# One projection for queries and keys, spread by transfers, and one load of the first batch in a two-layer attention kernel

## The chip, the cores and the metric

The kernel runs on one core of a Trainium2 chip, in one launch. The metric is the device time of that core in microseconds, the median of the runs; the profile is one more execution, recorded by the hardware profiler. "Granted clock" is the share of full speed that TensorE was allowed to run at.

## The reference

The input x is [4, 128, 64, 64] in float32: 4 batches of 128 channels by S = 4096 positions. Layer 0 is an attention over 1x1 convolutions with 64 channels for queries and keys:

```python
def _prelu(x, a):
    return jnp.where(x >= 0, x, a * x)
def _conv1x1(x, w, b, a):
    y = jnp.einsum('oc,nchw->nohw', w, x) + b[None, :, None, None]
    return _prelu(y, a)
e1 = _conv1x1(x, w1, b1, a1).reshape(N, -1, HW)     # queries, 64 channels
e2 = _conv1x1(x, w2, b2, a2).reshape(N, -1, HW)     # keys, 64 channels
asm = _conv1x1(x, wa, ba, aa).reshape(N, C, HW)     # values, 128 channels
score = jax.nn.softmax(jnp.einsum('nci,ncj->nij', e1, e2), axis=2)
out = jnp.einsum('nij,ncj->nci', score, asm)
...
x = x + _L0_conv_ref(_gn(x), ...)                   # _gn: group norm, 32 groups
t = _to_tokens(x)
t = t + _L1_attn_ref(_ln_t(t), Wq, Wk, Wv)          # layer 1: attention over tokens, D = 128
t = t + _L1_ffn_ref(_ln_t(t), gate_w, gate_b, weight1, weight2)   # routed experts
x = _from_tokens(t, x)
```

The change lies in layer 0 alone: in the group norm of the first batch, and in how e1 and e2 are made.

## The kernel before, in words

A batch is cut into 8 blocks of 512 positions (`BLK`), and the keys of a batch into 16 pairs of 128-position tiles. Everything is float32.

The work is a row of stages, `stage(b, layer, beside, then, ahead, pace)`, written out by hand at L767 and after: layer 0 of batch 0, layer 0 of batch 1, layer 1 of batch 0, layer 0 of batch 2, and so on. In a stage, `attention(b, layer)` goes over the 8 query blocks n and, for each, over 8 groups g of two pairs of keys. For a group, TensorE makes the scores (`ps`, L482), ScalarE their exponentials (`pt`, L491), and TensorE multiplies the group before with the values (`av`, L416 in layer 0, L444 in layer 1). VectorE adds up the exponentials in layer 0 (`sacc`, L503 and L506) and mixes them for layer 1 (L430 to L432). After the last group `finish_conv` or `finish_attn` ends the block in a few steps: in layer 0 a sum over the keys (`c`, L524; `pd`, L528), a reciprocal (L530), products and sums on GpSimd, and a store to DRAM (L535).

Python generators bring in what later stages need. Each step of `attention` advances one step of `beside` (statistics, keys and values of later batches), at g = 1 and after also the query of the next block (`coming`), and in the first block of queries up to three steps of `ahead`. The tile framework then orders the instructions of each engine and puts in the waits; each engine, and each queue that issues transfers, works through its own list in order.

What the change touches, with lines of the kernel before:

- `group_norm(b)`, L178: loads the 8 blocks of x (`g`, L96), takes statistics of each (`bn_stats`, L182), puts them together (L186), and gets mean and factor of each group of channels by two small products (L189, L199) with short VectorE operations between and after (L168 to L173, L191 to L194).
- `normed`, L215: one VectorE operation, (x - mean) * factor, on a 128x512 block.
- `conv_half`, L219: a product of 128x128 weights with the normalised block (`peq` for queries, `pek` for keys, both L222), and a copy with bias on ScalarE (L226). The 64 output channels stand twice in the weights (`w12`), so that both halves of the 128 partitions hold the same 64 rows.
- `prelu`, L207 and L209: two VectorE steps.
- `conv_keys(b)`, L231: for each block the load (`ck`), `normed`, `conv_half(1, ...)`, and the activation into the key tile `kA`, in two operations that write 64 partitions each: partitions 0 to 63 take the first tile of each pair, partitions 64 to 127 the second. Then four products for the values (`pa`, L256) and their activation into `vT`.
- `conv_query(b, n)`, L273: loads the block (`xq`, which is also the residual that the end of the block adds), `normed`, `conv_half(0, ...)`, activation into `q`.
- In the scores of layer 0 the upper 64 partitions of `kA` meet the upper 64 of `q`, and the lower the lower. That is why the query has to stand in both halves.

Loads go through SyncE's queue, those of the constants through ScalarE's. The loads of x for statistics, keys and layer 1 share four buffers (`xs`); normalised blocks (`xn`), `ye` and `te` have two each; `q` two; `xq` four. The large tiles of a batch (`kA`, `vT`) are in `seq`, two buffers each. The kernel opens with the statistics of batch 0, then the query of its first block, then the first stage, whose `ahead` is `conv_keys(0)` with six steps at once and three for each group.

Of the kernel before, what the change touches and what calls it, by code (L numbers as in the profile page):

```python
# [9 lines left out]
F32 = mybir.dt.float32  # L10
AF = mybir.ActivationFunctionType
# [4 lines left out]
P = 128  # L16
BLK = 512
# [9 lines left out]
def tile_unshifted(  # L27
# [14 lines left out]
    nc = tc.nc  # L42
    x = a["x"]
    B, C, S = x.shape
    E, D1, H = a["weight1"].shape
    O = a["weight2"].shape[2]
    CR = a["w12T"].shape[1] // 2
    assert C == P and D1 == P + 1 and O == P and 2 * CR == P and 2 * E == P and B == 4
    NB = S // BLK
    NJ = S // P  # L50
    SUB = BLK // P
# [5 lines left out]
    const = ctx.enter_context(tc.tile_pool(name="const", bufs=1))  # L57
# [18 lines left out]
    def ms_tile(name):  # L76
        return ps_ms.tile([P, BLK], F32, tag="ms", name=name)

    def block_tile(tag, name, bufs=2):
        pool = pools[of_pool.get(tag, "blk")]  # L80
        return pool.tile([P, BLK], F32, tag=tag, name=name, bufs=bufs)

    def dram_tile(shape, name):
        return dram.tile(shape, F32, tag=name, name=name)
# [6 lines left out]
    tokens = [[dram_tile([P, SUB, C], f"tk_{b}_{n}") for n in range(NB)] for b in range(B)]  # L91
    first_pair = dram_tile([P, S], "first_pair")

    def load_block(tag, src, name, bufs):
        t = block_tile(tag, name, bufs)
        nc.sync.dma_start(out=t, in_=src)  # L96
        return t

    def x_of(b, n):
        return x[b][:, bass.ts(n, BLK)]  # L100


    gn_x = [load_block("xs", x_of(0, n), f"g0_{n}", 4) for n in range(3)]

    def const_load(name, shape, src):
        t = const.tile(shape, F32, tag=name, name=name)
        nc.scalar.dma_start(out=t, in_=src)
        return t

    w12 = const.tile([P, 2, 2, CR], F32, tag="w12", name="w12")  # L110
    a12 = const.tile([P, 2], F32, tag="a12", name="a12")
    b12 = const.tile([P, 2], F32, tag="b12", name="b12")
    for i, al in enumerate(("a1", "a2")):
        for h in range(2):
            half = slice(h * CR, (h + 1) * CR)
            nc.scalar.dma_start(out=w12[:, i, h, :], in_=a["w12T"][:, bass.ts(i, CR)])
            nc.scalar.dma_start(out=b12[half, i : i + 1], in_=a["b12"][bass.ts(i, CR), :])
        nc.scalar.dma_start(out=a12[:, i : i + 1], in_=a[al].partition_broadcast(P))
    wa = const_load("wa_sb", [P, C], a["waT"])
    ba = const_load("ba_sb", [P, C], a["ba"].partition_broadcast(P))  # L120
    aa = const_load("aa_sb", [P, 1], a["aa"].partition_broadcast(P))
# [53 lines left out]

    gn = {}

    def group_norm(b, first=()):  # L178
        st = small.tile([P, NB, 6], F32, tag="gn_st", name=f"gn_st{b}")
        for n in range(NB):  # L180
            xb = first[n] if n < len(first) else load_block("xs", x_of(b, n), f"g{b}_{n}", 4)
            nc.vector.bn_stats(out=st[:, n, :], in_=xb)  # L182
            if n % 2 == 1:
                yield
        mv = small.tile([P, 2], F32, tag="gn_mv", name=f"gn_mv{b}")
        nc.vector.bn_aggr(out=mv, in_=st.rearrange("p n s -> p (n s)"))  # L186
        yield
        pm = ms_tile(f"gn_pm{b}")
        nc.tensor.matmul(pm[:, 0:1], lhsT=avg_g, rhs=mv[:, 0:1], start=True, stop=True)  # L189
        ab = const.tile([P, 2], F32, tag=f"gn{b}", name=f"gn{b}")  # L190
        nc.vector.tensor_copy(ab[:, 0:1], pm[:, 0:1])  # L191
        d = small.tile([P, 2], F32, tag="gn_d", name=f"gn_d{b}")
        nc.vector.tensor_sub(d[:, 0:1], mv[:, 0:1], ab[:, 0:1])
        nc.vector.scalar_tensor_tensor(  # L194
            d[:, 1:2], in0=d[:, 0:1], scalar=d[:, 0:1], in1=mv[:, 1:2], op0=ALU.mult, op1=ALU.add
        )
        yield
        pv = ms_tile(f"gn_pv{b}")
        nc.tensor.matmul(pv[:, 0:1], lhsT=avg_g, rhs=d[:, 1:2], start=True, stop=True)  # L199
        inv_sqrt(ab[:, 1:2], pv[:, 0:1], GN_EPS, 1, f"gn{b}")  # L200
        gn[b] = ab
        yield


    def prelu(outs, y, t, alpha):

        nc.vector.tensor_scalar(t, y, 0.0, alpha, op0=ALU.min, op1=ALU.mult)  # L207
        for o, part in outs:
            nc.vector.scalar_tensor_tensor(  # L209
                o, in0=part(y), scalar=0.0, in1=part(t), op0=ALU.max, op1=ALU.add  # L210
            )

    def normed(b, xb, name):
        xn = block_tile("xn", name)
        nc.vector.tensor_scalar(  # L215
            xn, xb, gn[b][:, 0:1], gn[b][:, 1:2], op0=ALU.subtract, op1=ALU.mult
        )
        return xn

    def conv_half(i, xn, name):  # L220
        pe = ms_tile(f"pe{name}")
        nc.tensor.matmul(  # L222
            pe, lhsT=w12[:, i].rearrange("p h c -> p (h c)"), rhs=xn, start=True, stop=True
        )
        y, t = block_tile("ye", f"ye{name}"), block_tile("te", f"te{name}")
        nc.scalar.activation(y, pe, AF.Identity, bias=b12[:, i : i + 1])  # L226
        return y, t

    keys, values = {}, {}

    def conv_keys(b):  # L231


        kA = seq.tile([P, NP, P], F32, tag="k", name=f"e2_{b}")
        vT = seq.tile([P, NJ, C], F32, tag="v", name=f"asm{b}")
        keys[b, 0], values[b, 0] = kA, vT
        xb = load_block("xs", x_of(b, 0), f"ck{b}_0", 4)
        for n in range(NB):
            xn = normed(b, xb, f"xk{b}_{n}")
            if n + 1 < NB:  # L240
                xb = load_block("xs", x_of(b, n + 1), f"ck{b}_{n + 1}", 4)
            yield
            y, t = conv_half(1, xn, f"k{b}_{n}")
            pairs = bass.ts(n, SUB // 2)

            def piece(h):
                rows = slice(h * CR, (h + 1) * CR)
                return kA[rows, pairs, :], lambda z: z[rows, :].rearrange(
                    "c (p h t) -> c p h t", h=2, t=P
                )[:, :, h, :]  # L250

            prelu([piece(0), piece(1)], y, t, a12[:, 1:2])
            yield
            pa = ms_tile(f"pa{b}_{n}")
            for s in range(SUB):
                nc.tensor.matmul(  # L256
                    pa[:, bass.ts(s, P)], lhsT=xn[:, bass.ts(s, P)], rhs=wa, start=True, stop=True
                )
            y2, t2 = block_tile("ye", f"ya{b}_{n}"), block_tile("te", f"ta{b}_{n}")
            y3 = y2.rearrange("p (s c) -> p s c", c=C)  # L260
            nc.vector.tensor_tensor(
                y3, pa.rearrange("p (s c) -> p s c", c=C),
                ba.unsqueeze(1).to_broadcast([P, SUB, C]), op=ALU.add,
            )
            prelu(
                [(vT[:, bass.ts(n, SUB), :], lambda z: z.rearrange("p (s c) -> p s c", c=C))],
                y2, t2, aa,
            )
            yield
# [2 lines left out]

    def conv_query(b, n):  # L273

        resid[b, 0, n] = xq = load_block("xq", x_of(b, n), f"xq{b}_{n}", 4)
        yield
        xn = normed(b, xq, f"xqn{b}_{n}")
        yield
        y, t = conv_half(0, xn, f"q{b}_{n}")
        q = block_tile("q", f"e1_{b}_{n}")  # L280
        prelu([(q, lambda z: z)], y, t, a12[:, 0:1])
        queries[b, 0, n] = q
        yield


# [395 lines left out]
    def run(gen):  # L681
        for _ in gen:
            pass
# [18 lines left out]
    def chain(*gens):  # L702
        for g in gens:
            yield from g
# [4 lines left out]
    def stage(b, layer, beside, then, ahead=None, pace=(6, 3)):  # L709

        coming = iter(())
        for k in range(pace[0]):
            next(ahead or iter(()), None)
        for n, g in attention(b, layer):
            step_after()
            if g == 1:
                coming = query(b, layer, n + 1) if n + 1 < NB else then and query(*then, 0)
                coming = coming or iter(())  # L720
            next(coming, None)
            if n == 0 and ahead:
                for _ in range(pace[1]):
                    next(ahead, None)
            else:
                next(beside, None)
        run(coming)
        run(beside)

    run(group_norm(0, gn_x))  # L730
    run(query(0, 0, 0))
    def take_from_seq(b):
        def take(what):
# [30 lines left out]
        weights(1, seq, "v")  # L764
        yield

    stage(0, 0, chain(group_norm(1), conv_keys(1), weights_qk()), (1, 0), ahead=conv_keys(0))  # L767
    stage(1, 0, chain(group_norm(2), attn_keys(0), mix_values(0)), (0, 1))
    stage(0, 1, chain(group_norm(3), conv_keys(2)), (2, 0))
    stage(2, 0, chain(done_after(route(0, take_from_seq(0))), attn_keys(1), mix_values(1)), (1, 1))  # L770
    stage(1, 1, conv_keys(3), (3, 0))
    stage(3, 0, chain(done_after(route(1, take_from_seq(1))), attn_keys(2), mix_values(2)), (2, 1))
    stage(2, 1, attn_keys(3), (3, 1))
    ends["prep"].close()
# [672 lines left out]
```

## Time and profile before

| | |
|---|---|
| time, median of 3 | 3559.84 us (3558.11 to 3560.43) |
| span of the profiled execution | 3558.6 us |
| mean granted clock | 0.984 |
| TensorE, first 20 us | 1.26 us busy |
| TensorE, 20 to 3390 us | 18 us idle in all |
| DMA, first 20 us | 216 GB/s |
| DMA, whole span | 40 GB/s |

A page of the profile gives busy time, share of the span and number of instructions of each engine; then the span in 40 slices, each digit a tenth of busy time. Groups of instructions have a line, an engine, an operation, what is written from what, shapes and number; after the bar the busy time, the mean duration in ns, and the idle time of the engine just before them with what ended it. A product in float32 shows as two records. Timelines give start and duration in us.

Where TensorE stands idle between the start and the end, it is in a few places: some 3 us at 58 to 64 us, 6 us at 562 to 571 us, and some 4 us each near 1290 and 2140 us. The last two slices are the experts and the final store, which the change does not touch.

### The profile page before, as it was taken

Reading aid. Unit: us, or ns where it says so; the run is one execution under the profiler, and the core shown is the slowest. Engines: PE = TensorE matmul, PEld = TensorE weight load, DVE = VectorE, ACT = ScalarE, POOL = GpSimd, SP = SyncE. Lnnn points to the kernel's source line nnn. Section 1 sums busy time; section 2 is a strip of 40 time slices with the busy share of each in tenths; the row PEclk is TensorE's granted clock in tenths of the full one; section 3 lists DMA queues with packets and bytes.
Section 4 is the critical chain, followed back from the end, with each engine's and each line's share of the span. In section 5 each row is a group of like instructions: output and inputs, shape, how many; then the busy total and the mean of one; then the engine's idle time right before and its main releaser. Section 6 shows DMA issues by size and latency. Waiting matters only on the chain.

```text
span 3558.6 us, 48815 instructions
## 1 busy us (share of the span) xinstructions
PE 3456.7 (97%) x19968; PEld 1631.2 (46%) x19968; DVE 2175.0 (61%) x4154; ACT 1339.3 (38%) x1555; POOL 508.6 (14%) x394
## 2 busy tenths in 40 slices
PE   7999999999999999999999999999999999999966
PEld 3444444444444445444444445444444444454432
DVE  7686576656665565766655566675665557555543
ACT  2333343333333343433333344443343334333330
POOL 0112243220000022421000003332100003000000
PEclk9999999999999999999999999999999999999977
DMA  3010011000000010100000001110100001010159
GB/s 102 24 48 13 13 36 54 15 15 22 21 19 10 19 39 18 42 24 19 24 16 19 10 19 58 34 34 12 39 22 19 13 16 42 10 66 7 36 197 355
DMA packets 75450, 142.37 MB, mean 40 GB/s; under 512 B 8593, under 2 KB 9361, under 8 KB 74961
## 3 DMA queue, kind: packets, MB, share of 16 engines
q1 hardware_dynamic: 67952, 130.18, 10.9%
q10 hardware_dynamic: 7264, 8.98, 0.7%
q8 instruction: 158, 2.59, 0.3%
q14 instruction: 76, 0.61, 0.1%
HBM read 95.10 MB, written 44.04 MB: 39 GB/s over the span
## 4 chain that ended last, share of the span: by engine, by line
PE 94%; DVE 3%; DMA 2%; ACT 1%; issue 0%; POOL 0%; SPq 0%; ACTq 0%; DVEq 0%; POOLq 0%
PE ps L482 38%; PE av L416 23%; PE av L444 22%; PE l_c L312 1%; DMA g<-in_x_dram 1%; PE pv L562 1%; PE pg L591 1%; PE peq L222 1%; PE pd L528 1%; PE pq L386 1%; PE pa L256 1%; PE pek L222 1%; PE ph L828 1%; PE x_c L312 1%; PE po L858 1%; PE l_t L289 0%
## 5 line engine op out<-in xcount | busy, mean ns | idle before, releaser
L491 ACT ACTIVATE pt<-ps 128x1024 f32<-128x1024 f32 x1024 | 1021.4, 1023 | 1293.6 <-PE ps L482 1214.0
L482 PE MATMUL ps<-q,t 128*64 128x512 f32 x4096 | 936.3, 597 | 0.0
L416 PE MATMUL av<-pt,asm 64*128 64x512 f32 x4096 | 925.8, 591 | 0.9 <-ACT sw L546 0.9
L506 DVE TENSOR_TENSOR sacc<-sacc,pt 128x1024 f32<-128x1024 f32 x448 | 615.5, 1374 | 262.7 <-ACT pt L491 239.9
L430 DVE TENSOR_TENSOR tt<-pt 128x512 f32<-128x512 f32 x512 | 358.2, 700 | 493.7 <-ACT pt L491 474.3
L444 PE MATMUL av<-pt,tt 128*64 128x256 f32 x3072 | 636.5, 379 | 0.0
L416 PEld LDWEIGHTS av<-pt,asm 64*128 64x128 f32 x4096 | 405.6, 188 | 480.3 <-issue 466.6
L444 PE MATMUL av<-tt,mixed 128*64 128x256 f32 x2048 | 525.9, 380 | 0.0
L482 PEld LDWEIGHTS ps<-q,t 128*64 128x64 f32 x4096 | 281.2, 137 | 519.3 <-issue 479.6
L482 PE MATMUL ps<-e,e 64*128 64x512 f32 x2048 | 505.0, 611 | 7.2 <-ACT pt L491 7.1
L444 PEld LDWEIGHTS av<-pt,tt 128*64 128x64 f32 x3072 | 352.6, 137 | 289.4 <-issue 142.2
L169 POOL TENSOR_TENSOR l_y<-l_v,mhalf 128x4 f32<-128x4 f32 x64 | 74.3, 1161 | 1758.2 <-DVE l_v L168 1757.9
L444 PE MATMUL av<-tt,tt 128*64 128x256 f32 x1024 | 304.9, 380 | 0.0
L444 PE MATMUL av<-pt,mixed 128*64 128x256 f32 x1024 | 304.6, 379 | 0.0
L482 PEld LDWEIGHTS ps<-e,e 64*128 64x128 f32 x2048 | 190.9, 189 | 234.8 <-issue 216.2
L444 PEld LDWEIGHTS av<-tt,mixed 128*64 128x64 f32 x2048 | 280.8, 137 | 2.4
L431 DVE TENSOR_TENSOR pt<-tt,pt 128x256 f32<-128x256 f32 x512 | 220.0, 430 | 14.8
L432 DVE TENSOR_TENSOR tt<-pt 128x256 f32<-128x256 f32 x512 | 220.2, 431 | 14.2
L444 PEld LDWEIGHTS av<-pt,mixed 128*64 128x64 f32 x1024 | 139.4, 137 | 72.1
L444 PEld LDWEIGHTS av<-tt,tt 128*64 128x64 f32 x1024 | 140.3, 137 | 1.7 <-DVE tt L432 0.2
L530 DVE RECIPROCAL inv<-pd 128x512 f32<-128x512 f32 x32 | 107.4, 3356 | 36.9 <-PE pd L528 36.9
L525 POOL TENSOR_TENSOR all_sum<-all_sum,c 128x512 f32<-128x512 f32 x32 | 46.1, 1440 | 532.2 <-DVE c L524 532.2
(192 smaller groups left out, 2167.1 us busy)
## 6 DMA issues: line engine op xcount, KB each, us to landing
w<-in_weight_dram SPq DMA_DIRECT2D x32, 1024.0 KB, 12.0
x<-xp SPq DMA_DIRECT2D x64, 256.0 KB, 2.2
g<-in_x_dram SPq DMA_DIRECT2D x32, 256.0 KB, 2.8
xq<-in_x_dram SPq DMA_DIRECT2D x32, 256.0 KB, 3.1
ck<-in_x_dram SPq DMA_DIRECT2D x32, 256.0 KB, 2.9
ak<-x SPq DMA_DIRECT2D x32, 256.0 KB, 2.8
xT<-xT SPq DMA_DIRECT2D x32, 256.0 KB, 2.9
xr<-xT SPq DMA_DIRECT2D x32, 256.0 KB, 2.7
```

Of the source, the lines that this page charges most:

```text
L169: nc.gpsimd.tensor_tensor(y[:, :k], v[:, :k], mhalf[:, :k], op=ALU.pow)
L222: nc.tensor.matmul(pe, lhsT=w12[:, i].rearrange("p h c -> p (h c)"), rhs=xn, start=True, stop=True)
L312: nc.tensor.transpose(pt[:, bass.ts(s, P)], src[:, s, :], ident)
L416: nc.tensor.matmul(avs[b, 0, n][:, r, :], lhsT=values[b, 0][rows, j, :], rhs=pt[rows, h, :], start=(j == 0), stop=(j == NJ - 1),)
L430: nc.vector.tensor_sub(tt[:, 0:2, :], p4[:, :, 1, :], p4[:, 0, :, :])
L431: nc.vector.tensor_add(p4[:, 0, 1, :], tt[:, 1, :], p4[:, 0, 0, :])
L432: nc.vector.tensor_sub(tt[:, 2, :], p4[:, 1, 0, :], p4[:, 0, 1, :])
L444: nc.tensor.matmul(av[bass.ts(half, HC), bank, slot, :], lhsT=lhsT, rhs=rhs, start=first, stop=final, skip_group_check=True,)
L482: nc.tensor.matmul(ps[part, h, :], lhsT=key[:, part], rhs=q[rows, :], start=True, stop=True,)
L491: nc.scalar.activation(pt, ps, AF.Exp, scale=scale)
L506: nc.vector.tensor_add(sums[b, n], sums[b, n], pt)
L530: nc.vector.reciprocal(r, pd)
```

## The change

The queries and the keys of a block come from one product: the weights now hold w1 in columns 0 to 63 and w2 in columns 64 to 127, so partitions 0 to 63 of the product are the query and 64 to 127 the key. One ScalarE copy with bias and one activation follow for both (`b12` and `a12` hold one value for each partition). The halves that attention needs are then made by transfers from SyncE's queue: two from the key half of `ye` into the two halves of `kA`, and one of the query half to a DRAM tile `e1[b][n]`, from which `conv_query` later loads both halves of `q`. The second normalisation, product, copy and activation per block go.

For batch 0, x is loaded once as a whole into a buffer of `seq`, in four parts on two queues, and serves the statistics and the projections; before, the statistics and the keys each loaded their own blocks. The first three steps of `conv(0)` (block 0) now run ahead of the first query, and the first stage then takes three steps at once instead of six.

```diff
+    e1 = [[dram_tile([CR, BLK], f"e1_{b}_{n}") for n in range(NB)] for b in range(B)]
...
-    gn_x = [load_block("xs", x_of(0, n), f"g0_{n}", 4) for n in range(3)]
+    first_x = seq.tile([P, S], F32, tag="v", name="first_x")
+    for i, q in enumerate((nc.sync, nc.scalar, nc.sync, nc.scalar)):
+        part = bass.ts(i, S // 4)
+        q.dma_start(out=first_x[:, part], in_=x[0][:, part])
...
+    w12 = const_load("w12", [P, 2 * CR], a["w12T"])
+    b12 = const_load("b12", [P, 1], a["b12"])
+    a12 = const.tile([P, 1], F32, tag="a12", name="a12")
...
-    def group_norm(b, first=()):
+    def group_norm(b, first=None):
...
-            xb = first[n] if n < len(first) else load_block("xs", x_of(b, n), f"g{b}_{n}", 4)
+            if first is None:
+                xb = load_block("xs", x_of(b, n), f"g{b}_{n}", 4)
+            else:
+                xb = first[:, bass.ts(n, BLK)]
...
-            y, t = conv_half(1, xn, f"k{b}_{n}")
...
-            prelu([piece(0), piece(1)], y, t, a12[:, 1:2])
+            pe = ms_tile(f"pe{b}_{n}")
+            nc.tensor.matmul(pe, lhsT=w12, rhs=xn, start=True, stop=True)
+            y, t = block_tile("ye", f"ye{b}_{n}"), block_tile("te", f"te{b}_{n}")
+            nc.scalar.activation(y, pe, AF.Identity, bias=b12)
+            prelu([(y, lambda z: z)], y, t, a12)
+            y4 = y[CR:, :].rearrange("c (p h t) -> c p h t", h=2, t=P)
+            for h in range(2):
+                nc.sync.dma_start(
+                    out=kA[h * CR : (h + 1) * CR, bass.ts(n, SUB // 2), :], in_=y4[:, :, h, :]
+                )
+            nc.sync.dma_start(out=e1[b][n], in_=y[:CR, :])
...
-        resid[b, 0, n] = xq = load_block("xq", x_of(b, n), f"xq{b}_{n}", 4)
-        yield
-        xn = normed(b, xq, f"xqn{b}_{n}")
-        yield
-        y, t = conv_half(0, xn, f"q{b}_{n}")
-        q = block_tile("q", f"e1_{b}_{n}")
-        prelu([(q, lambda z: z)], y, t, a12[:, 0:1])
-        queries[b, 0, n] = q
+        resid[b, 0, n] = load_block("xq", x_of(b, n), f"xq{b}_{n}", 4)
+        queries[b, 0, n] = q = block_tile("q", f"e1_{b}_{n}")
+        for h in range(2):
+            nc.sync.dma_start(out=q[h * CR : (h + 1) * CR, :], in_=e1[b][n])
...
-    run(group_norm(0, gn_x))
+    run(group_norm(0, first_x))
+    first_conv = conv(0, first_x)
+    for _ in range(3):
+        next(first_conv)
     run(query(0, 0, 0))
...
-    stage(0, 0, chain(group_norm(1), conv_keys(1), weights_qk()), (1, 0), ahead=conv_keys(0))
+    stage(0, 0, chain(group_norm(1), conv(1), weights_qk()), (1, 0), ahead=first_conv, pace=(3, 3))
```

In the other stages `conv_keys(b)` becomes `conv(b)` in the same place.

## The prediction

> **What bounds the kernel now.** I read the page's busy table and its 40 slices first, then the groups of instructions on TensorE, the waits of TensorE between 51 and 3390 us, and last the timeline at the start and around single products. The page, with TensorE's row of the slices:
>
> ```profile
> span 3558.6 us, 48815 instructions
> PE 3456.7 (97%) x19968; PEld 1631.2 (46%) x19968; DVE 2175.0 (61%) x4154; ACT 1339.3 (38%) x1555; POOL 508.6 (14%) x394
> ...
> PE   7999999999999999999999999999999999999966
> ```
>
> TensorE is full in every slice but the first and the last two. VectorE (61%) and ScalarE (38%) have room in every stage. So an instruction taken off TensorE between those ends is worth its whole time, and one taken off another engine nothing, unless TensorE was waiting for it. The waits of TensorE from 51 to 3390 us (waiter, engine waited for, us in total, times, longest) say where it was:
>
> ```profile
> PE ps L482 <- ACT pt L491: 7.1, 2, 3.6
> PE pd L528 <- DVE c L524: 4.1, 1, 4.1
> PE pek L222 <- DVE xk L215: 1.9, 1, 1.9
> ```
>
> The whole answer sums to some 18 us. What the change removes, in the groups on TensorE (64 records are 32 products; the last column is the idle time before them):
>
> ```profile
> L222 PE MATMUL peq<-xqn,w 128*128 128x512 f32 x64 | 36.6, 654 | 2.3 <-DVE xqn L215 2.3
> ```
>
> Busy time counts overlap with the next product, so I price a product by the start of what follows it. The timeline of TensorE (start, us, ...) shows one query product alone between value products (av) and scores (ps), a step without one, and a query product beside a key product:
>
> ```profile
> 50.32 1.13 PE L222 MATMUL peq<-xqn,w 128*128 128x512 f32 x2
> 51.28 1.02 PE L222 MATMUL pek<-xk,w 128*128 128x512 f32 x2
> ...
> 97.50 3.60 PE L416 MATMUL av<-pt,asm 64*128 64x512 f32 x16
> 100.93 1.88 PE L482 MATMUL ps<-e,e 64*128 64x512 f32 x8
> 102.65 3.60 PE L416 MATMUL av<-pt,asm 64*128 64x512 f32 x16
> 106.18 1.13 PE L222 MATMUL peq<-xqn,w 128*128 128x512 f32 x2
> 107.23 1.99 PE L482 MATMUL ps<-e,e 64*128 64x512 f32 x8
> ```
>
> From av to ps takes 3.43 us without it (97.50 to 100.93) and 4.58 with it (102.65 to 107.23): 1.15 us. Beside another full product it is 51.28 - 50.32 = 0.96 us.
>
> The start, the other thing that the change touches, in the timeline of all engines:
>
> ```profile
> 15.27 0.37 DVE L186 BATCH_NORM_AGGREGATE gn_mv<-gn_st 128x2 f32<-128x48 f32 x1
> ...
> 19.28 0.55 DVE L215 TENSOR_SCALAR xqn<-xq,gn 128x512 f32<-128x512 f32 x1
> ...
> 26.51 1.99 PE L482 MATMUL ps<-e,e 64*128 64x512 f32 x8
> ```
>
> The statistics end at 15.3 us, the first normalised block is there at 19.8, the first score starts at 26.51. A second hole follows, in TensorE's timeline:
>
> ```profile
> 60.66 1.92 PE L222 MATMUL pek<-xk,w 128*128 128x512 f32 x2 [1.93 <-DVE xk L215]
> 63.47 2.07 PE L256 MATMUL pa<-wa_sb,xk 128*128 128x128 f32 x8 [0.89 <-DVE ya L261]
> 65.48 3.04 PE L482 MATMUL ps<-e,e 64*128 64x512 f32 x8
> ```
>
> Here VectorE stood in batch 1's statistics, waiting for their loads. The usual step is pek 0.96, pa 0.98, ps 1.82; here it ran from 58.66 to 68.35, 9.7 us for 3.8: some 6 us lost.
>
> **What the Trainium skill says.** "TensorE: Matmul & The Clock Gate", section "What's actually happening": after an idle window of about 3.4 us TensorE falls to half its clock until it has been busy for as long. The trace agrees: the slow records above follow idle time, and after the 4.1 us wait for c at 562 us a score group shows 3.79 us instead of 1.99. "DMA: Bandwidth & Descriptors", section "Anatomy of one DMA", has about 2.0 us fixed for a transfer and says that semaphore waits are taken on the issuing sequencer; the trace has 2.2 us for a 256 KB store (x from xp) and 2.8 to 3.1 for a load, so I use those. The same page, "Issuing engines are not separate DMA queues": a second issuing queue saves issue time, not bandwidth. The trace moves 190 GB/s in the first 10 us and 242 in the next, with single slices to 374, so I expect no doubling.
>
> **The change part by part.** *Query products.* 32 leave. The key product keeps its shape (128x128 weights, 512 columns) and its price. Leaving out blocks 0 and 1 of batch 0, which belong to the start below, 30 go. By their neighbours in the order of TensorE, of the 24 behind the first that I looked through, 13 stand alone and 11 beside another product; in that proportion, with block 1 among the latter, I take 17 at 1.15 and 13 at 0.96: 19.6 + 12.5 = **32.0 us**. Ends: 30 x 0.96 = 28.8 and 30 x 1.15 = 34.5.
>
> *Other engines.* VectorE loses per block a normalisation (0.54), the two steps of the activation (0.49 + 0.69) and 0.86 - 0.69 for the halves of the key; ScalarE loses 0.69. Hidden behind TensorE, so nothing.
>
> *Spread of keys and queries.* Per block SyncE now issues two key transfers, a store of the query half and later two loads of it: three or four tenths of a us each to issue, landing in 2.2 to 3 us. Keys of batches 1 to 3 are used a stage later and queries about 45 us after their load can start (their slot is free when the scores of two blocks before are done), so both hide. In the first block of batch 0 the key of block n is needed about one step later: from the start of its product to the scores that use it are a whole step and two products, 7.3 + 2 = 9.3 us; key product, ScalarE and VectorE took 4.05 us (35.73 to 39.78), issue and landing 3: 7 of 9.3. Hidden. The buffer of y is now held until three transfers have read it, so ScalarE's copy for a later block waits on SyncE's queue, and the exponentials and then TensorE stand behind it. SyncE's queue is in order and has stores in it that wait for GpSimd; by the order of the built kernel the worst place (batch 1, block 3, behind a store of block 2's output) has about 3 us to spare. I count 0, and up to 10 us (one hole like that at 562 us) for the range.
>
> *Start.* Batch 0 is loaded once, in four 512 KB parts, without waiting for buffers: 2.1 MB at 190 to 370 GB/s after 2.8 us land at about 8.5 to 13 us; I take 10.5, so the eighth statistic ends at 11.5 (before: 15.2). But the built order puts four loads and statistics of batch 1 inside the chain that makes the mean and the factor on VectorE: one ahead of the aggregate, one ahead of the copy of the mean, two ahead of the variance. Each stands behind first_x and two residual blocks in SyncE's queue. Issued from 10.5 us and landing in about 3.3, each pair behind the one before: 13.8 and 14.8, then 16 and 18.3. Aggregate at 14.9, copy 15.6, variance 19.2; the rest takes 1.6 as before (17.67 to 19.28), so the first block is normalised at 21.5 (before 19.8). Three more statistics of batch 1 stand before the activation of block 0 (24.1), then ya, xk, te, ta and ye at 0.69, 0.54, 0.49, 0.49, 0.69 with gaps: 27.4. The query store goes out third, lands at 30.9. Its loads stand in SyncE's queue behind the keys of block 1, whose activation ends at about 30.9 as well; issued at 31.8, landed at 34.6. **First score at about 35 us, 8.5 later.** TensorE idles from 27.8 to 31.6 in it and may be cold again.
>
> On the other side, by then two key and one value product more are done (2 x 0.96 + 0.98 = 2.9 us), the query product of block 1 is gone (0.96), and the hole at 58 to 68 us is gone, because batch 1's statistics are done (6). I add 2 us for the second pair of scores, which wait for exponentials behind a held y. From the first score to the first score of block 1 the old kernel takes 79.08 - 26.51 = 52.6 us; the new one 52.6 - 6 - 2.9 - 1.0 + 2 = 44.7, so it arrives at 79.7 against 79.08. **Sum for the start: +0.6 us.** Ends: loads and statistics landing without waits, first score at 30, -4.4; each load 1 to 2 us later, first score at 41, +6.6.
>
> *Sum:* 3559.84 + 0.6 - 32.0 = 3528.4; I say 3529.
>
> **The rivals.**
> 1. *The start gains outright:* one load instead of two, statistics done 4 us sooner, and batch 1's loads in time. First score at 26.5 with the hole gone: -8 in place of +0.6, 3520. For it: the DMA rate above 300 GB/s in single slices. Against: the order of VectorE, which now mixes two batches.
> 2. *Holes from held buffers and SyncE's queue:* one to two holes of 6 to 10 us, as at 58 and 562 us, in the stages that make keys: 3535 to 3548. For it: both old holes come from just such loads ahead of compute on an in-order engine. Against: the 3 us and more to spare counted above.
> 3. *Nothing comes of it:* three to four such holes eat the 32 us: 3552 to 3567.
> 4. *Slower:* the round trip of each query block lands on the path. A store and a load are 2.2 + 2.8 = 5 us; if only half showed on each of 32 blocks, 80 - 32 = +48: 3608. Against: each is issued about a block (some 45 us) ahead. If only batch 0's eight blocks showed it all, 40 - 32 = +8: 3568.
>
> **How the numbers follow.** The forecast has 0.62, rival 1 0.14, rival 2 0.14, rival 3 0.05 (most of it within 0.2%), rival 4 0.05. 0.2% is 7 us, so forecast and rivals 1 and 2 all count as faster: with a little of 3, 0.91; same 0.04; slower 0.05. The range runs from 3518 (rival 1 with 34.5 saved) to 3543 (rival 2 with one and a half holes); it leaves out about 0.13, the worse part of 2, and 3 and 4.
>
> **What would show it.** Right: 32 matmuls of 128x512 fewer on TensorE and a busy time some 30 us lower; no wait for the loads of batch 1 at 58 us; waits of TensorE in the middle still near 18 us; the first score between 30 and 41 us; the first score of block 1 at 75 to 86. Wrong: TensorE waiting for e1, e2 or y in the middle, groups of scores at 3 to 4 us after them, or ScalarE's first activations waiting for transfers after 80 us; then the held buffer is the term that I missed. A first score past 41 us would put the miss into the start.

## The result, and the profile after

The changed kernel takes 3535.3 us (median of four, 3534.6 to 3536.2) beside 3559.9 us before (3558.1 to 3560.4): 24.6 us less, ratio 0.9932 with a 95% interval of 0.9915 to 0.9949. Forecast were 3529.0 us and a range of 3518 to 3543.

The page of the changed kernel, with TensorE's row of the slices:

```profile
span 3533.4 us, 48826 instructions
PE 3421.0 (97%) x19904; PEld 1623.1 (46%) x19904; DVE 2115.3 (60%) x4026; ACT 1318.9 (37%) x1523; POOL 518.3 (15%) x394
...
PE   7999999999999999999999999999999999999965
```

TensorE has 64 records (32 matmuls) less and is 35.7 us less busy. It is still the bound. Its waits between 51 and 3365 us in the changed kernel (waiter, engine waited for, us in total, times, longest):

```profile
PE ps L483 <- ACT pt L492: 7.9, 3, 3.6
PE pd L529 <- DVE c L525: 4.8, 1, 4.8
PE pa L261 <- DVE ya L266: 3.4, 1, 3.4
PE l_c L313 <- DVE tt L305: 3.4, 4, 1.7
...
```

With two small ones more they sum to 21.6 us, against 18.0 before. The two waits in the hole at 58 us (1.9 and 0.9) are gone; the wait of 3.4 us of pa for ya is new, and the waits for tt, pt and c are 3.0 us longer together. The products that are left, in the groups, and TensorE's timeline at the place where a query product stood alone before, with the row that follows that query product in the kernel before:

```profile
L248 PE MATMUL pe<-xk,w 128*128 128x512 f32 x64 | 37.4, 667 | 4.7 <-DVE xk L222 2.7 <-ACT ye L250 1.2 <-DVE ya L266 0.8
```

```profile
103.59 3.60 PE L417 MATMUL av<-pt,asm 64*128 64x512 f32 x16
107.03 1.88 PE L483 MATMUL ps<-e,e 64*128 64x512 f32 x8
108.74 3.60 PE L417 MATMUL av<-pt,asm 64*128 64x512 f32 x16
```

```profile
109.06 3.60 PE L416 MATMUL av<-pt,asm 64*128 64x512 f32 x16
```

From av to ps are 3.44 us, where 4.58 were; and the next value products follow the scores after 1.71 us, where after a query product they followed after 1.83 (107.23 to 109.06). So from one group of value products to the next are 5.15 us, where 6.41 were, and a product alone is worth 1.26 us.

The start in the timeline of the changed kernel:

```profile
12.64 0.35 DVE L193 BATCH_NORM_AGGREGATE gn_mv<-gn_st 128x2 f32<-128x48 f32 x1
...
19.69 1.00 DVE L222 TENSOR_SCALAR xk<-first_x,gn 128x512 f32<-128x512 f32 x2
...
35.27 3.02 PE L483 MATMUL ps<-e,e 64*128 64x512 f32 x8
```

**Where the time went.** Each query block of layer 0 ends with one product pd, and each of layer 1 with pg. The start of these 64 products, matched between the two traces, tells how far the changed kernel has come ahead. The first five:

| end of query block | before, us | after, us | difference | step |
|---|---|---|---|---|
| batch 0, block 0 | 94.62 | 95.57 | +0.95 | |
| block 1 | 140.62 | 140.31 | -0.31 | -1.26 |
| block 2 | 189.92 | 188.75 | -1.17 | -0.86 |
| block 3 | 240.87 | 243.57 | +2.70 | **+3.87** |
| block 4 | 290.74 | 292.58 | +1.84 | -0.86 |

From block 4 on it gains mostly in steps of 0.86 or 1.26 (in the two blocks that end at 563 and 613 us it loses 0.54 and gains 2.82, together about the worth of two products), stands still where a stage has no query product to lose, and ends at -25.67 (3418.37 and 3392.70 for the last product pg). The sum: +0.95 at the start; 16 products alone at 1.26 and 14 beside another at 0.87, -32.3; a new hole in block 3, where a gain of 1.26 was due and 3.87 were lost, +5.1; two places (1494 and 2334 us) where a step was only 0.16 and 0.14, because TensorE waited 0.55 us for tt instead, +1.4; and some small ones, -0.8, of which 0.65 in the block that ends at 1307 us, where no query product was. So 0.95 - 32.3 + 5.1 + 1.4 - 0.8 = -25.65.

The hole, in VectorE's and then TensorE's timeline of the changed kernel:

```profile
210.03 0.68 DVE L189 BATCH_NORM_STATS2 gn_st<-g 128x6 f32<-128x512 f32 x1
215.80 0.69 DVE L189 BATCH_NORM_STATS2 gn_st<-g 128x6 f32<-128x512 f32 x1 [5.09 <-DMA g<-in_x_dram]
...
216.82 0.63 DVE L266 TENSOR_TENSOR ya<-pa,ba_sb 128x512 f32<-128x512 f32 x1
```

```profile
217.50 1.37 PE L261 MATMUL pa<-wa_sb,xk 128*128 128x128 f32 x8 [3.42 <-DVE ya L266]
218.80 3.41 PE L483 MATMUL ps<-e,e 64*128 64x512 f32 x8
```

VectorE stands 5.09 us in the eighth statistic of batch 2, and ya, which frees the PSUM tile for the next value half, stands behind it. TensorE waits 3.42 us, and its next scores run at 3.41 us instead of 1.99. The kernel before had the same wait on VectorE, but with ya ahead of it, and there it cost nothing:

```profile
200.94 0.68 DVE L261 TENSOR_TENSOR ya<-pa,ba_sb 128x512 f32<-128x512 f32 x1
...
211.88 0.69 DVE L182 BATCH_NORM_STATS2 gn_st<-g 128x6 f32<-128x512 f32 x1 [2.79 <-DMA g<-in_x_dram]
```

In the changed kernel ScalarE also stood, in its copy to y, for the spread that still read the buffer:

```profile
213.35 0.69 ACT L250 ACTIVATE ye<-pe,b 128x512 f32<-128x512 f32 x1 [7.99 <-DMA e<-ye]
```

And the load of that statistic was the last of a row on SyncE: the store of x1 waits for GpSimd (xp ends at 209.02), the spread of block 3, a residual block, then the load:

```profile
209.05 0.33 SPq L536 DMA_DIRECT2D x<-xp  x1
209.42 1.32 SPq L254 DMA_DIRECT2D e<-ye  x2
210.79 0.61 SPq L257 DMA_DIRECT2D e<-ye  x1
211.44 0.58 SPq L98 DMA_DIRECT2D xq<-in_x_dram  x1
212.12 0.39 SPq L98 DMA_DIRECT2D g<-in_x_dram  x1
```

The row holds the load back by 1.4 us and not by more: the load also needs a buffer, and that comes free when the seventh statistic ends, at 210.71. The five statistics loads before it (186.39 to 200.48) were each issued 0.02 to 0.03 us after a statistic had ended.

So two theories: A, the held y stalls ScalarE, its exponentials and so TensorE (the prediction's mechanism); B, the late load stalls VectorE and with it ya. B has two parts, the row in the queue and the place of the statistic on VectorE.

### The profile page after: what moved, and what is told of

Its sections match the earlier page's. It is cut to its first block, busy times and chain, and to the rows that moved or that the text cites. A ratio compares the mean times of both kernels' runs of the same rounds, so it can differ in the third digit from the quotient of the medians.

```text
span 3533.4 us, 48826 instructions
## 1 busy us (share of the span) xinstructions
PE 3421.0 (97%) x19904; PEld 1623.1 (46%) x19904; DVE 2115.3 (60%) x4026; ACT 1318.9 (37%) x1523; POOL 518.3 (15%) x394
## 4 chain that ended last, share of the span: by engine, by line
PE 92%; DMA 3%; DVE 2%; ACT 1%; POOL 1%; issue 0%; SPq 0%; ACTq 0%; DVEq 0%; POOLq 0%
PE ps L483 38%; PE av L417 23%; PE av L445 22%; DMA g<-in_x_dram 1%; PE l_c L313 1%; PE pv L563 1%; PE pg L592 1%; PE pa L261 1%; PE pd L529 1%; PE pe L248 1%; PE pq L387 1%; DMA y<-x 1%; PE x_c L313 1%; PE pp L656 0%; PE l_t L290 0%; DMA w<-in_weight_dram 0%
```

## The experiments

The kernels below ran in three groups (1 to 4, 5 to 8, 9 to 11), each beside the kernel before, with medians of 3558.0, 3558.6 and 3557.5 us for it. So times of different groups are compared to about 2 us; where less matters I use the ends of query blocks. The changed kernel and the runs that alter only the order, the queue or the products later on end block 0 at 94.2 to 96.0 us, and runs 1 and 6, which have the same start as each other, at 93.0 and 95.3. So some 2 us there is scatter.

**1. y in buffers of its own** (theory A against B).

```diff
-            y, t = block_tile("ye", f"ye{b}_{n}"), block_tile("te", f"te{b}_{n}")
+            y, t = block_tile("ye", f"ye{b}_{n}"), block_tile("te", f"te{b}_{n}", 1)
...
-            y2, t2 = block_tile("ye", f"ya{b}_{n}"), block_tile("te", f"ta{b}_{n}")
+            y2, t2 = block_tile("ya", f"ya{b}_{n}", 1), block_tile("te", f"ta{b}_{n}", 1)
...
```

Here and below `...` stands for lines of an edit that are left out. y keeps two buffers; y2 now has one of its own, and the temporaries of both share one.

> The changed kernel with y in two buffers of its own (y2 and the two temporaries share the rest), so that the spread no longer holds a buffer that the value half needs. Question: what made the new hole of 5.1 us at 214 to 222 us (query block 3 of batch 0). Theory A, the held y stalls ScalarE and so the exponentials: the hole is gone, 3530 us (3529 to 3532). Theory B, VectorE stands in the eighth statistic of batch 2, whose load is queued on SyncE behind a store that waits for GpSimd and behind the spread; the order on both engines is not touched here: the hole stays, 3534 to 3537 us.

Measured: 3534.1 us (3531.4 to 3536.5). ScalarE no longer waits for a transfer there, it waits for TensorE, in ScalarE's and then TensorE's timeline and wait list of this kernel:

```profile
206.20 0.69 ACT L250 ACTIVATE ye<-pe,b 128x512 f32<-128x512 f32 x1 [3.40 <-PE pe L248]
...
218.81 1.02 ACT L492 ACTIVATE pt<-ps 128x1024 f32<-128x1024 f32 x1 [9.60 <-PE ps L483]
```

```profile
PE pa L261 <- DVE ya L266: 3.2, 1, 3.2
```

The hole is there as before; block 3 even takes 1.2 us longer. Theory A falls.

**2. The store of x1, the residual loads and the spread from GpSimd's queue** (the stores everywhere, the loads from batch 0's fifth block, the spread from batch 1 on), so that the statistics loads stand in a row on SyncE.

```diff
-    resid[b, 0, n] = load_block("xq", x_of(b, n), f"xq{b}_{n}", 4)
+    resid[b, 0, n] = load_block(
+        "xq", x_of(b, n), f"xq{b}_{n}", 4, nc.gpsimd if b or n > 3 else None
+    )
...
-    nc.sync.dma_start(out=x1[b][n], in_=xp)
+    nc.gpsimd.dma_start(out=x1[b][n], in_=xp)
...
+    queue = nc.gpsimd if b else nc.sync
...
```

`queue` then issues the three transfers of the spread.

> The changed kernel with layer 0's stores of x1, its xq loads (from the fifth on) and the spread of batches 1 to 3 issued from GpSimd's queue instead of SyncE's. The eight statistics loads of batch 2 then stand one after another on SyncE with nothing ahead that waits. Theory B (the load is late): the hole at 214 to 222 us is gone, 5.1 us, 3530 us (3528 to 3532). Theory A (y is held): y comes free no earlier, rather later, as its transfer now stands behind GpSimd's additions: hole as before or larger, 3535 to 3540 us. Third possibility, GpSimd's additions get late by issuing: new waits on xp in layer 0, slower than 3540.

Measured: 3537.9 us. The hole shrinks by 3.8 us (block 3 takes 51.05 us, 54.82 in the changed kernel), the wait of pa to 1.3 us:

```profile
PE pa L262 <- DVE ya L267: 1.3, 1, 1.3
```

The 1.3 that is left is VectorE still standing 3.29 us in the eighth statistic: its load was issued at 208.98, when the statistic before it had just ended (208.95) and freed the buffer, and landed 3.2 us later. So the queue is not all of it: the order on VectorE leaves the last load no time. The total gets worse, because 7.6 us are lost again later, 3.1 of them in one block at 2286 to 2334 us, where TensorE waits 2.1 us for tt and runs slow after it (shown in the last section). GpSimd's timeline shows why. It computes `l_y`, from which VectorE makes tt, and now does so behind the issues:

```profile
1454.55 0.63 POOL L539 DMA_DIRECT2D x<-xp  x1 [0.30 <-POOL xp L538]
1455.18 0.55 POOL L98 DMA_DIRECT2D xq<-in_x_dram  x1
1455.74 1.03 POOL L173 TENSOR_TENSOR l_y<-l_v,mhalf 128x4 f32<-128x4 f32 x1
```

In the changed kernel `l_y` follows the addition to xp at once. Here it comes 1.5 us later, and at this place TensorE waits 2.10 us for tt instead of 0.55.

**3. The same, with the spread left on SyncE.**

```diff
-    queue = nc.gpsimd if b else nc.sync
+    queue = nc.sync
```

> As the one before, but the spread stays on SyncE, so that the load of the eighth statistic stands behind the spread of block 3 alone and no longer behind GpSimd's addition. Theory B in its full form (store and spread each cost their part): the load is issued 2 to 2.5 us earlier, the hole shrinks to 2.5 to 3 us, 3532.5 to 3533.5 us. If the store alone is to blame: as the one before, 3530. If the store plays no part: 3535.

Measured: 3544.6 us, against 3532.5 to 3533.5 expected, a miss. The load was issued at 210.83, 1.3 us earlier than 212.12, not 2 to 2.5, and the hole shrank by 0.9 us; the wait of pa is 2.7 us. SyncE's queue and VectorE in this kernel:

```profile
209.40 0.60 SPq L258 DMA_DIRECT2D e<-ye  x1
210.83 0.33 SPq L98 DMA_DIRECT2D g<-in_x_dram  x1
```

```profile
210.13 0.68 DVE L189 BATCH_NORM_STATS2 gn_st<-g 128x6 f32<-128x512 f32 x1
215.25 0.69 DVE L189 BATCH_NORM_STATS2 gn_st<-g 128x6 f32<-128x512 f32 x1 [4.44 <-DMA g<-in_x_dram]
```

The queue was free from 210.00, and the load went out 0.02 us after the seventh statistic ended (210.81). So here, as in run 2, it waited for its buffer and for nothing in the queue. It then took 4.4 us to land, where it took 3.2 in run 2; why was not tested. The rest is lost later, in the same blocks as in the run before (8.0 us from the end of block 3 on), though the spread is back on SyncE. So those losses come with the store and the residual loads on GpSimd.

**4. The query products back on TensorE alone**, 30 of them, into PSUM tiles that nobody reads.

```diff
+        if b or n > 1:
+            spare = ms_tile(f"pq{b}_{n}")
+            nc.tensor.matmul(spare, lhsT=w12, rhs=resid[b, 0, n], start=True, stop=True)
...
```

> The changed kernel with the 30 query products of blocks beyond the first two put back on TensorE alone: each product of 128x128 with the residual block goes to a spare PSUM tile that nobody reads; no activation, no VectorE work, no transfer comes with it, and the result is not used. Theory (the gain is TensorE's time): 30 x (0.87 to 1.26) = 26 to 38 us slower than the changed kernel, about 3535 + 32 = 3567 us (3562 to 3572). Rival (a third or more of the gain came from the VectorE, GpSimd and ScalarE work that went with the products): at most 3557 us.

Measured: 3569.2 us, 33.9 more than the changed kernel, as expected. The timeline shows the product's price:

```profile
103.03 3.60 PE L422 MATMUL av<-pt,asm 64*128 64x512 f32 x16
106.56 1.12 PE L288 MATMUL pq<-xq,w 128*128 128x512 f32 x2
107.61 1.99 PE L488 MATMUL ps<-e,e 64*128 64x512 f32 x8
109.43 3.60 PE L422 MATMUL av<-pt,asm 64*128 64x512 f32 x16
```

Again 4.58 from av to ps. In the ends of query blocks nearly all steps are 1.26 and 0.85 to 0.91 as before; the large exception is block 3, +7.3, where the same hole is larger (a wait of 7.1 us for ya: the spare tile takes its turn in the two PSUM tiles that these products share, so the product before the value half has to wait for ya already). So some 6 of the 33.9 us are the hole. Beside the kernel before, the ends of all blocks but block 0 and block 3 keep their steps to 1.6 us in all. So the gain is TensorE's time; for what VectorE and ScalarE were spared, 1.6 us outside these two blocks are left at most.

**5. One edge of order on VectorE:** the eighth statistic of batch 2 behind the value half of block 3 of batch 1.

```diff
-            nc.vector.bn_stats(out=st[:, n, :], in_=xb)
+            with tc.issue_after(last_prelu[1, 3]) if (b, n) == (2, 7) else nullcontext():
+                nc.vector.bn_stats(out=st[:, n, :], in_=xb)
```

`last_prelu[1, 3]` is the instruction that ends that value half on VectorE; the edge sets the order alone.

> The changed kernel with one edge of order on VectorE: the eighth statistic of batch 2 is issued behind the value half of block 3 of batch 1 instead of ahead of it. Two instructions change places, queues and buffers stay. Theory B in the form that the runs so far leave (VectorE stands in a statistic whose load comes late, and y2 stands behind it): the hole at 214 to 222 us is gone altogether, 3530 us (3529 to 3531.5). If the late load also held up something else (the spread, ScalarE's wait of 8 us for y): a hole of 2 us or more stays, 3532 to 3535 us.

Measured: 3531.5 us (3529.7 to 3531.6). VectorE and ScalarE in this kernel:

```profile
210.37 0.68 DVE L190 BATCH_NORM_STATS2 gn_st<-g 128x6 f32<-128x512 f32 x1
210.97 0.67 DVE L268 TENSOR_TENSOR ya<-pa,ba_sb 128x512 f32<-128x512 f32 x1
...
216.09 0.69 DVE L190 BATCH_NORM_STATS2 gn_st<-g 128x6 f32<-128x512 f32 x1 [2.87 <-DMA g<-in_x_dram]
```

```profile
213.70 0.69 ACT L252 ACTIVATE ye<-pe,b 128x512 f32<-128x512 f32 x1 [7.93 <-DMA e<-ye]
```

ya comes at 210.97 instead of 216.82, TensorE has no wait at all between 203 and 224 us, and block 3 takes 5.12 us less: the whole hole. ScalarE waits for y as long as before (7.93), and it costs nothing. That settles it: B, and in B the place of the statistic on VectorE. The load goes out as late as before, behind the same row (212.47), and costs nothing. Of the 5.1 us, 0.9 are lost again in the block that ends at 613 us (the cause was not looked for); the last block ends 3.1 us earlier than in the changed kernel, and the medians, of two groups, are 3.8 us apart.

**6. Both: the edge and y's own buffers.**

```diff
-            y, t = block_tile("ye", f"ye{b}_{n}"), block_tile("te", f"te{b}_{n}")
+            y, t = block_tile("ye", f"ye{b}_{n}"), block_tile("te", f"te{b}_{n}", 1)
+            with tc.issue_after(last_prelu[1, 3]) if (b, n) == (2, 7) else nullcontext():
```

> The edge of order and y's own buffers together. The own buffers brought 1 to 2.5 us at the start (93.0 against 95.6 us at the end of query block 0, of which one us or so can be scatter) and gave 1.2 us back in the hole that the edge removes: 3528 us (3526.5 to 3530). If the gain of the own buffers was scatter: as the edge alone, 3530.

Measured: 3531.4 us, as the edge alone. The gain at the start of run 1 (93.0 us at the end of block 0) is not repeated (95.3); it was scatter. So holding y costs nothing that these runs can measure.

**7. The first load alone**, both products kept, and **8. one product and the spread alone**, with the old loads of batch 0.

```diff
# 7, against the kernel before
-    gn_x = [load_block("xs", x_of(0, n), f"g0_{n}", 4) for n in range(3)]
+    first_x = seq.tile([P, S], F32, tag="v", name="first_x")
+    for i, q in enumerate((nc.sync, nc.scalar, nc.sync, nc.scalar)):
+        part = bass.ts(i, S // 4)
+        q.dma_start(out=first_x[:, part], in_=x[0][:, part])
...
# 8, against the changed kernel: the same lines the other way round
```

> The kernel before with only the first load changed (batch 0 loaded whole by two queues, used for statistics and key blocks); the two products per block stay. The prediction's working has the hole at 58 to 68 us, 6 us, go with this part: 3553 to 3555 us, and the end of query block 0 at 88 to 90 us instead of 94.6. Rival (the start is bound by VectorE and ScalarE, not by the loads): 3557 to 3560 us.

> The changed kernel with the old loads of batch 0 (three blocks for statistics ahead, the others and the projection blocks one by one); one product per block and the spread stay. If the first load is worth 6 us at the start: 3541 us, and the end of query block 0 near 101 us. If it is worth nothing once the query products are gone: 3534 to 3537 us. The 32 us of the products stay in both.

Measured: 3554.95 us for the load alone (ratio 0.9991, 0.9982 to 1.0000), 3540.1 for the product alone (0.9950, 0.9933 to 0.9966); 3541 was expected for the product alone. The ends of block 0, where 88 to 90 us were expected for run 7 and some 101 for run 8:

| | two products | one product and spread |
|---|---|---|
| old loads | 94.62 (before) | 102.74 (run 8) |
| whole first load | 91.88 (run 7) | 95.57 (changed) |

The whole load is worth 2.7 us with the old products and 7.2 with the new one; the single product with its spread costs 8.1 us at the start without the load and 3.7 with it. In run 8 the hole at 58 us is back and a wait for the query's loads with it, in TensorE's timeline:

```profile
34.15 5.29 PE L477 MATMUL ps<-e,e 64*128 64x512 f32 x12 [1.30 <-DMA e<-e]
...
62.18 1.87 PE L255 MATMUL pa<-wa_sb,xk 128*128 128x128 f32 x8 [1.54 <-DVE ya L260]
64.95 4.32 PE L477 MATMUL ps<-e,e 64*128 64x512 f32 x8 [0.90 <-ACT ye L244]
```

In run 7 there is no wait of TensorE from 27 to 75 us. Beside the scatter of some 2 us, the 2.7 us are small, the others are not. So at the start the load pays for most of the latency that the spread brings. In the whole times the two parts nearly add: 3.7 us less for the load and 18.5 for the product, 22.2 together, against 24.6 for both. Run 7 has no hole in block 3 and run 8 has one of 3.2 us, so the hole came with the one product and its spread and not with the load. Whether by the transfers or by the new order on VectorE, these two runs don't tell apart.

**9 to 11. What sets the new start.** All three with the edge of run 5. In 9 the first query tile is filled straight from y, without the way through DRAM; in 10 batch 1's statistics are issued behind the first normalisation of batch 0; 11 has both.

```diff
# 9: the first query
+            if b == 0 and n == 0:
+                queries[0, 0, 0] = q0 = block_tile("q", "e1_0_0")
+                for h in range(2):
+                    nc.gpsimd.dma_start(out=q0[h * CR : (h + 1) * CR, :], in_=y[:CR, :])
...
# 10: every statistic of batch 1
+            behind = {2: last_prelu.get((1, 3)) if n == 7 else None, 1: last_prelu.get("xk")}.get(b)
+            with tc.issue_after(behind) if behind else nullcontext():
+                nc.vector.bn_stats(out=st[:, n, :], in_=xb)
...
+        last_prelu.setdefault("xk", ins.ins)
```

`last_prelu["xk"]` is the first normalisation, of block 0 of batch 0.

> The edge of order of the eighth statistic, and the first query tile alone filled by two transfers straight from y on GpSimd's queue instead of a store to DRAM and two loads back. The first score waited for those loads (issued 30.8 us, first score 35.3 us). If the round trip through DRAM sets the start: first score at 31 to 32 us, and the gain of 3 us or so kept to the end, 3528 us. If VectorE's chain of the next blocks sets it: first score earlier by some us, end of query block 0 within 1 us of the run without, 3530.5 to 3532.

> The edge of order of the eighth statistic, and batch 1's statistics issued on VectorE behind the first normalisation of batch 0. Four of them stood in the chain to the first product in the changed kernel (12.0, 14.7, 16.2 and 17.5 us). If they delay the start: first product at 16.5 to 18 us instead of 20.3, and 2 to 4 us less in all, 3528 us. If the hole at 58 to 68 us comes back, because batch 1's scales come late: 3531 to 3537.

> The edge of order with both changes of the start, the direct first query and the late statistics of batch 1. If both causes add: 3 + 3 us off the edge alone, 3525.5 us (3524 to 3528). If one of the two hides the other: 3528. If the start is bound elsewhere: 3531.

| run | first product | first score | end of block 0 | time, us |
|---|---|---|---|---|
| 5, edge alone | 20.62 | 35.68 | 95.97 | 3531.5 |
| 9, direct query | 19.32 | 29.08 | 90.12 | 3527.3 (3526.1 to 3529.7) |
| 10, late statistics | 15.63 | 31.37 | 91.32 | 3526.1 (3526.0 to 3526.2) |
| 11, both | 15.83 | 25.89 | 92.23 | 3524.3 (3521.9 to 3526.7) |

Run 9 gains 4.2 us on run 5 and run 10 5.4, and both end block 0 more than the scatter earlier (5.9 and 4.7 us). So both the way through DRAM and the four foreign statistics were on the path of the start. Whether they add is not settled. By the medians, which are of two groups, run 11 gains 7.2 of the 9.6 us, with four times from 3521.9 to 3526.7. The execution that was profiled is the slowest of these. In it the first score is 10 us earlier than in run 5, but TensorE waits before it, and its first two groups of scores take 5.19 and 3.79 us instead of 1.99:

```profile
24.22 1.13 PE L253 MATMUL pe<-xk,w 128*128 128x512 f32 x2 [1.81 <-ACT ye L255]
25.89 5.19 PE L492 MATMUL ps<-e,e 64*128 64x512 f32 x8 [0.54 <-DMA e<-ye]
31.01 2.07 PE L271 MATMUL pa<-wa_sb,xk 128*128 128x128 f32 x8
33.01 3.79 PE L492 MATMUL ps<-e,e 64*128 64x512 f32 x8
```

With 3524.3 us (ratio to before 0.9904, 0.9887 to 0.9920) run 11 is the fastest, 11 us below the changed kernel; against run 10 it can't be told apart (the times overlap).

## Why the prediction was right, and where it was not

The time lies in the range and 6.3 us above the forecast. By its steps:

*Query products: right, the size in part by luck.* 32.0 us were forecast, 32.3 found. The two prices erred in opposite ways: alone 1.15 forecast and 1.26 found, because the value products that follow the next scores also come some 0.1 us later after such a product; beside another product 0.96 forecast and 0.87 found. That the saving lies on TensorE is shown by run 4.

*Other engines: nothing, right.* Run 4 puts back TensorE's part only, and outside blocks 0 and 3 all but 1.6 us of the saving goes.

*Start: +0.6 forecast, +0.95 found,* within the scatter of some 2 us. The hole of 6 us that should go went: run 7 has its first score 3.2 us later than before (29.68 against 26.51) and ends block 0 2.7 earlier, so 5.9. The first score came at 35.27, forecast about 35, but partly by luck. The chain on VectorE was faster than worked out (aggregate 12.6 and not 14.9, first normalised block ready by 20.3, when its product starts, not 21.5; the loads of the query issued at 30.8, not 31.8). In its place TensorE, in order, did a value half at 2.05 us and a key product at 2.07 before the score, both at about half their usual speed (1.05 and 1.13 us from 50 us on). That the foreign statistics and the way through DRAM set this start, as the prediction had it, is shown by runs 9 and 10. One label was wrong: the scores at 79.08 us are the last pair of block 0, not the first of block 1, which begins at 84.22; the same pair was meant on both sides (80.02 after), so the comparison stands.

*Spread: this step failed.* "The worst place (batch 1, block 3, behind a store of block 2's output) has about 3 us to spare. I count 0, and up to 10 us for the range." The place was the right one, and the cost was 5.1 us, not 0. The mechanism given with it was not the one: it had ScalarE's copy standing for a held y and the exponentials behind it. ScalarE did stand there for 8 us, and runs 1, 5 and 6 show that this costs nothing. What counted was a load that the working did not have in its account: the last statistics load of the next batch comes late, and in the changed kernel's order VectorE has that statistic ahead of ya. The row with the spread held the load back by 1.4 us beyond the moment at which its buffer came free. The spread's issues took 0.6 us each and not the three or four tenths of the working. Runs 2 and 3 take that delay away and keep waits of 1.3 and 2.7 us; run 5 keeps the row, moves the statistic, and has no wait. So the place on VectorE is what makes the hole, and the row adds to it. The prediction had looked for who waits for the spread, and not for what VectorE would have behind a late load. Rival 2, holes from held buffers and SyncE's queue, came true with one hole, smaller than its 6 to 10 us, and without the held y as a cause.

*Small waits:* another 1.4 us are the two places where a wait of 0.55 us for tt took part of a removed product's place.

So forecast 3559.84 + 0.6 - 32.0 = 3528.4; with the measured terms, 0.95 - 32.3 + 5.1 + 1.4 - 0.8 = -25.65 by the traces, and -24.6 by the medians.

Of what should show it, the wait at 58 us is gone and the first score is in its bounds; the waits in the middle are 21.6 us and not 18, of which 3.4 are the new hole. A group of scores at 3.41 us behind it was named as the sign of a wrong step, and it was that. ScalarE waiting for a transfer was named as the sign of the held buffer; it came too, and pointed to the wrong cause.

## What to carry to other kernels

Where new transfers are put on a queue, list what stands behind them in that queue (here a load of another batch, 1.4 us later), and for each of those loads the instruction that stands in an engine for it and what that engine has behind it; the victim need not have anything to do with the transfers. A load that needs the buffer of the work just before it is late without any queue. A work item of a later stage that fills an engine's free time (here a statistic of the next batch) should be issued behind the current stage's own work of the same moment, not ahead of it: one edge of order brought back 5.1 us in its block and 3.1 us at the end. Before issues are moved to an engine that also computes, list what waits for its results. On an engine that is the bound, price a removed product by the start of what follows it, and take the step after as well.

## What the runs showed of the hardware

*A wait of 2 us can cost twice or only once.* The prediction cited the Trainium skill, "TensorE: Matmul & The Clock Gate", "What's actually happening", for an idle window of about 3.4 us before TensorE slows down, and found the trace to agree. It agrees for the 4.1 us wait, but the traces show less too: 1.93 us of idle at 60.66 us in the kernel before are followed by slow records, 1.28 us in run 2 (213.95 us) by none. And the same idle time goes both ways, in TensorE's timeline of run 2:

```profile
1458.00 1.09 PE L316 MATMUL l_c<-ident,tt 128*128 128x128 f32 x4 [2.10 <-DVE tt L308]
1459.03 1.99 PE L486 MATMUL ps<-e,e 64*128 64x512 f32 x8
...
2300.15 1.24 PE L316 MATMUL l_c<-ident,tt 128*128 128x128 f32 x4 [2.11 <-DVE tt L308]
2301.32 3.41 PE L486 MATMUL ps<-e,e 64*128 64x512 f32 x8
```

The first wait cost 1.6 us against the changed kernel, the second 3.1. The same section says that the window in which activity is counted runs freely; that would let the same idle time fall on either side, but no run here tests it.

*Issuing from GpSimd takes its time:* 0.55 to 0.63 us for one transfer and 1.19 for two in run 2, next to products and sums of 1.3 to 2.3 us. With the store of x1 and a residual load there, what GpSimd computes next came 1.5 us later, and 7.6 us were lost in other blocks.
